# A decoder layer on one core: scores on four 32-row strips, values in one run, and a fixed order of products on TensorE

## The chip, the core and the metric

The kernel runs on one core of a Trainium2 chip. A core has TensorE (PE; its weight loads are shown apart, as PEld), VectorE (DVE), ScalarE (ACT), GpSimd (POOL) and SyncE (SP), which here only issues DMAs. TensorE writes its results into PSUM, eight banks of 128 partitions by 512 fp32 numbers; DVE and ACT read PSUM, POOL does not. The metric is the device time of one execution in microseconds, the median of the runs.

## The reference

Two sequences of 2048 tokens with 512 features go through three sublayers, each followed by a residual sum and a layer norm.

```
x = layernorm(x + ssm(x))                   # state-space layer, 16 heads of 32
x = layernorm(x + cross_attention(x, ctx))  # 16 heads of 32, 77 context tokens
x = layernorm(x + slots(x))                 # dispatch to 16 slots, 16 experts, combine
```

The change is in the second line. Its attention is

```
q = x@q_w + q_b;  k = ctx@k_w + k_b;  v = ctx@v_w + v_b       # per head 32 wide
att = softmax(causal(q @ k.T / sqrt(32)))                      # [token, 77] per head
x2  = layernorm(x + (att @ v) @ o_w + o_b)
```

and the same stage also computes the dispatch part of the third line: a running softmax over the tokens for 128 rows (16 slots times 16 heads, in two halves of 128) and the sums `Z` of `x2` weighted by it.

## The kernel before

Four stages follow one another. The first is the state-space layer; between its products, `setup()` computes the keys and values. The second, the attention stage, goes over 16 tiles of 256 tokens, each handled as two halves `s` of 128 tokens. The third runs the 16 experts, whose 192 MB of weights are streamed in 1 MB slabs by SP's queue. The last combines and writes the output.

Products that need more precision are split: an operand is kept as a high part in the format fp32r and a low remainder, and `three` adds high·high, high·low and low·high. These are single TensorE instructions. The plain fp32 products `uu`, `y`, `up` and `qp` appear in the trace as two instructions each; transposes are single ones.

In the attention stage the work of a tile `n` is cut into functions, which the text names by letters where the change does. `load` fetches the tokens and the first layer's output; `scaled` (POOL and ACT) prepares them. `out_proj` (O, per half) is 12 products with 512 columns, a residual sum and the layer norm's chain of small DVE and ACT instructions. `x1_transposed` (X, per half) is four transposes and the split. `queries` (Q, per half of the features) makes two groups of 12 products with 256 columns, both into one PSUM tile `qq`; behind each group ACT writes `qh` (L787) and DVE writes `ql` (L788) from that group's half of the tile. `weigh` (W) makes the scores of four heads: three products into one bank of `sc`, then the softmax on DVE and ACT, and a multiplication by the reciprocal on POOL (L820). `gather` (G) transposes the four heads' probabilities; `values` (V) multiplies them with the values. `o_proj` (P, per half) is 12 products with 512 columns and the second layer norm; `x2_transposed` (Y), `dispatch` (D, 24 products with 256 columns), `p_transposed` (T) and `collect` (C, twice six products with 512 columns) belong to the slots.

The keys are stored block-diagonally: for a group of four heads the right operand has 4·77 = 308 columns, and row strip `r` (32 rows, the features of head `r`) is non-zero only in its own 77 columns. One product over all 128 rows thus gives four heads' scores:

```
for k, (l, r) in enumerate(((qh, kbh[b]), (qh, kbl[b]), (ql, kbh[b]))):
    mm(sc[:, 0:4 * S], l[:, hg % 2, ss], r[:, hg, :], k == 0, k == 2)
```

Per tile there are 2 halves and 4 head groups, so 24 such products. `setup()` builds the block-diagonal keys in four blocks of two groups each: a POOL memset of `kf`, four DVE copies of 32 partitions (L443), an ACT cast and a POOL subtraction. In `values` every head's product uses 32 weight columns and writes its own 32 partitions, so that four heads use four column strips of the array; four heads make eight instructions.

The order of the calls comes from `plan` (eight lists, one tile's period), with hand-made lists for the `head` and the `drain`. The functions are called in that order, but the framework that builds the program then schedules every engine's instructions itself: it may move instructions of one engine past one another where no data dependence forbids it, and the queues of the engines hold the result, in a fixed order. Dependences on PSUM are kept by the framework.

PSUM in this stage: one bank `y`, two each for `mm`, `tr` and `sc`. `mm` serves O, Q, P, D and C in turn.

The experts' slabs `0` to `9` and `A` to `M` lie on memory that the attention stage partly still uses; `first` gives the order in which they are filled the first time, and `dwc` two slabs for two other weights (default `KL`).

Of the kernel before, what the change touches and what calls it, by code (L numbers as in the profile page):

```python
# [16 lines left out]
S = 77  # L17
NE, FF = 16, 2048
# [4 lines left out]
NT = T // TB  # L23
# [11 lines left out]
DEFPLAN = [  # L35
    ["W", "V", ["scaled", 0, 0], ["x2_transposed", 3, 1], ["queries", 1, 0], "G"],
    ["W", "V", ["scaled", 0, 1], ["dispatch", 3], "G"],
    ["W", "V", ["o_proj", 2, 0], "G"],
    ["W", "V", ["p_transposed", 3], ["queries", 1, 1], "G"],
    ["L", "W", "V", ["x2_transposed", 2, 0], ["out_proj", 0, 0], "G"],  # L40
    ["W", "V", ["out_proj", 0, 1], "G"],
    ["W", "V", ["x1_transposed", 0, 0], ["o_proj", 2, 1], "G"],
    ["W", "V", ["x1_transposed", 0, 1], ["collect", 3], "G"]]
# [33 lines left out]
def weave(flows, depth, lag):  # L77
# [3 lines left out]
    while flows or live:  # L81
# [4 lines left out]
        for f in list(live):  # L86
# [6 lines left out]
TUNED = {'plan': [['W', ['x2_transposed', 3, 1], 'V', 'G'], ['V', 'W', 'G', ['scaled', 0, 0]],  # L93
          ['G', ['out_proj', 0, 0], ['queries', 1, 0], 'W', 'V', ['dispatch', 3]], ['W', ['o_proj', 2, 0], ['queries', 1, 1], 'G', 'V'],
          ['G', 'V', 'W', ['scaled', 0, 1], ['x2_transposed', 2, 0]], ['V', ['p_transposed', 3], 'W', 'G'],
          ['W', 'V', ['out_proj', 0, 1], ['x1_transposed', 0, 0], 'G'],
          ['V', ['x1_transposed', 0, 1], ['o_proj', 2, 1], 'L', 'G', 'W', ['collect', 3]]],
 'E': {'uf': 2,
# [15 lines left out]
 'lg': 1,  # L114
 'lv': 2,
 'dv': [1, 3],
 'first': 'ABCD067451892GH3JIFEKLM',
# [63 lines left out]
 'head': [['load', 0], ['scaled', 0, 0], ['out_proj', 0, 0], ['load', 1], ['scaled', 0, 1], ['scaled', 1, 0], ['x1_transposed', 0, 0],  # L181
          ['out_proj', 0, 1], ['out_proj', 1, 0], ['x1_transposed', 0, 1], ['queries', 0, 0], ['queries', 0, 1], ['weigh', 0, 0, 0], ['load', 2],
          ['weigh', 0, 0, 2], ['gather', 0, 0, 0], ['scaled', 1, 1], ['weigh', 0, 0, 1], ['values', 0, 0, 0], ['out_proj', 1, 1], ['gather', 0, 0, 2],
          ['x1_transposed', 1, 0], ['gather', 0, 0, 1], ['values', 0, 0, 1], ['weigh', 0, 0, 3], ['x1_transposed', 1, 1], ['weigh', 0, 1, 0],
          ['values', 0, 0, 2], ['gather', 0, 1, 0], ['weigh', 0, 1, 1], ['weigh', 0, 1, 2], ['scaled', 2, 0], ['out_proj', 2, 0], ['gather', 0, 0, 3],
          ['queries', 1, 0], ['weigh', 0, 1, 3], ['values', 0, 0, 3], ['gather', 0, 1, 1], ['o_proj', 0, 0], ['gather', 0, 1, 2], ['values', 0, 1, 0],
          ['queries', 1, 1], ['scaled', 2, 1], ['weigh', 1, 0, 0], ['gather', 0, 1, 3], ['x1_transposed', 2, 0], ['weigh', 1, 0, 1],
          ['values', 0, 1, 1], ['values', 0, 1, 2], ['values', 0, 1, 3], ['x2_transposed', 0, 0], ['gather', 1, 0, 0], ['weigh', 1, 0, 2],
          ['values', 1, 0, 0], ['out_proj', 2, 1], ['gather', 1, 0, 1], ['load', 3], ['values', 1, 0, 1], ['weigh', 1, 0, 3], ['o_proj', 0, 1],
          ['x1_transposed', 2, 1], ['gather', 1, 0, 2], ['x2_transposed', 0, 1], ['weigh', 1, 1, 0], ['values', 1, 0, 2], ['gather', 1, 0, 3],  # L190
          ['scaled', 3, 0], ['values', 1, 0, 3], ['weigh', 1, 1, 1], ['gather', 1, 1, 0], ['out_proj', 3, 0], ['weigh', 1, 1, 2], ['queries', 2, 0],
          ['gather', 1, 1, 1], ['values', 1, 1, 0], ['dispatch', 0], ['o_proj', 1, 0], ['queries', 2, 1], ['weigh', 1, 1, 3], ['gather', 1, 1, 2]],
 'drain': [['values', 12, 1, 1], ['gather', 12, 1, 3], ['values', 12, 1, 2], ['weigh', 13, 0, 0], ['scaled', 14, 1], ['x2_transposed', 12, 0],
           ['values', 12, 1, 3], ['weigh', 13, 0, 1], ['p_transposed', 11], ['gather', 13, 0, 0], ['x1_transposed', 14, 0], ['weigh', 13, 0, 2],
           ['values', 13, 0, 0], ['out_proj', 14, 1], ['gather', 13, 0, 1], ['values', 13, 0, 1], ['x1_transposed', 14, 1], ['load', 15],
           ['o_proj', 12, 1], ['gather', 13, 0, 2], ['weigh', 13, 1, 0], ['weigh', 13, 0, 3], ['weigh', 13, 1, 1], ['values', 13, 0, 2],
           ['collect', 11], ['x2_transposed', 12, 1], ['gather', 13, 0, 3], ['gather', 13, 1, 0], ['values', 13, 0, 3], ['scaled', 15, 0],
           ['out_proj', 15, 0], ['gather', 13, 1, 1], ['weigh', 13, 1, 2], ['values', 13, 1, 0], ['dispatch', 12], ['queries', 14, 0],
           ['weigh', 13, 1, 3], ['gather', 13, 1, 2], ['scaled', 15, 1], ['o_proj', 13, 0], ['queries', 14, 1], ['values', 13, 1, 1],
           ['gather', 13, 1, 3], ['values', 13, 1, 2], ['weigh', 14, 0, 0], ['x2_transposed', 13, 0], ['p_transposed', 12], ['values', 13, 1, 3],  # L200
           ['weigh', 14, 0, 1], ['gather', 14, 0, 0], ['weigh', 14, 0, 2], ['values', 14, 0, 0], ['out_proj', 15, 1], ['x1_transposed', 15, 0],
           ['gather', 14, 0, 1], ['values', 14, 0, 1], ['x1_transposed', 15, 1], ['o_proj', 13, 1], ['gather', 14, 0, 2], ['weigh', 14, 0, 3],
           ['collect', 12], ['x2_transposed', 13, 1], ['weigh', 14, 1, 0], ['gather', 14, 0, 3], ['values', 14, 0, 2], ['values', 14, 0, 3],
           ['weigh', 14, 1, 1], ['queries', 15, 0], ['gather', 14, 1, 0], ['gather', 14, 1, 1], ['weigh', 14, 1, 2], ['dispatch', 13],
           ['values', 14, 1, 0], ['weigh', 14, 1, 3], ['o_proj', 14, 0], ['queries', 15, 1], ['gather', 14, 1, 2], ['values', 14, 1, 1],
           ['gather', 14, 1, 3], ['values', 14, 1, 2], ['x2_transposed', 14, 0], ['values', 14, 1, 3], ['weigh', 15, 0, 0], ['p_transposed', 13],
           ['weigh', 15, 0, 1], ['o_proj', 14, 1], ['gather', 15, 0, 0], ['weigh', 15, 0, 2], ['values', 15, 0, 0], ['gather', 15, 0, 1],
           ['weigh', 15, 0, 3], ['gather', 15, 0, 2], ['x2_transposed', 14, 1], ['values', 15, 0, 1], ['collect', 13], ['weigh', 15, 1, 0],
           ['weigh', 15, 1, 1], ['values', 15, 0, 2], ['weigh', 15, 1, 2], ['gather', 15, 0, 3], ['values', 15, 0, 3], ['gather', 15, 1, 0],
           ['gather', 15, 1, 1], ['dispatch', 14], ['values', 15, 1, 0], ['weigh', 15, 1, 3], ['o_proj', 15, 0], ['gather', 15, 1, 2],  # L210
           ['values', 15, 1, 1], ['gather', 15, 1, 3], ['x2_transposed', 15, 0], ['values', 15, 1, 2], ['values', 15, 1, 3], ['p_transposed', 14],
           ['o_proj', 15, 1], ['collect', 14], ['x2_transposed', 15, 1], ['dispatch', 15], ['p_transposed', 15], ['collect', 15]],
 'pme': 0,
 'b1': 27,
# [3 lines left out]
 'x2': 2,  # L218
 'zt': 2,
 'qb': 2}  # L220
# [3 lines left out]
def tile_decoder(ctx, tc, a, out, dbg=None, upto=9, opt=None):  # L224
# [56 lines left out]
    kbh, kbl = ([kv_[b].tile([128, 4, 4 * S], FR, name=f"kb{t}{b}") for b in range(B)] for t in "hl")  # L281
# [11 lines left out]
    with ExitStack() as st:  # L293
# [121 lines left out]
        def setup():  # L415
# [20 lines left out]
            for b in range(B):  # L436
                for h in range(2):
                    m2 = slice(2 * h, 2 * h + 2)
                    kf = sb.tile([128, 2, 4, S], FP, tag="sw", bufs=2, name="kf")
                    pool.memset(kf, 0.0)  # L440
                    for r in range(4):
                        sr = slice(32 * r, 32 * r + 32)
                        dve.tensor_copy(kf[sr, :, r, :], kst[sr, m2, b * S:b * S + S])  # L443
                    split(kbh[b][:, m2].rearrange("p m (r s) -> p m r s", s=S), kbl[b][:, m2].rearrange("p m (r s) -> p m r s", s=S), kf, pool)
                    yield
# [254 lines left out]

    with ExitStack() as st:
        psb = {tag: st.enter_context(tc.tile_pool(name="b_" + tag, bufs=n, space=PSUM, reuse_waits="tile"))
               for tag, n in (("y", 1), ("mm", 2), ("tr", 2), ("sc", 2))}
        sbq, sb1, sb0 = (st.enter_context(tc.tile_pool(name=nm, bufs=1, side="right", reuse_waits="tile"))
                         for nm in ("b_q", "b_x1T", "b_in"))
        sbz, sbx, sb = (st.enter_context(tc.tile_pool(name=nm, bufs=1, side="right", reuse_waits="tile"))
# [125 lines left out]
        def values(n, s, hg):  # L832
            b = n // NT
            if hg == 0:
                ts[n]["y", s] = PT("y", bufs=1)
# [95 lines left out]
        def period(p):  # L931

            for q8, items in enumerate(PLAN):
                for it in items:
# [8 lines left out]
                    if 0 <= op_[1] < N:  # L943
                        yield op_
# [650 lines left out]
```

## Time and profile before

| | us |
|---|---|
| median of three runs | 1507.3 (1503.42 to 1508.44) |
| the profiled execution: its own time | 1507.68 |
| its span, first to last instruction | 1505.3 |
| PE busy in the span | 1351.7 (90%) |
| DVE busy | 912.4 (61%) |
| ACT busy | 620.1 (41%) |
| POOL busy | 447.5 (30%) |
| first product of the attention stage starts | 315.4 |
| last product of the attention stage ends | about 923 |

The profiled execution took 2.4 us more than its span, and 0.4 us more than the median. The span's PE share is an average over stages: the state-space stage ends near 315 us, the attention stage runs to about 923 us, the experts to about 1400 us. In the third, the DMA engines move 408 GB/s on average and are busy 99% of the time from 925 to 1400 us; in the attention stage they move 59 GB/s.

In the lists of groups a line names the source line, engine, operation and tile (out<-in); in the timeline the first column is the start and the second the duration in us, and a bracket gives the engine's idle time before the instruction and what released it. Matmuls are pipelined, so that their durations overlap: the price of one is the distance from its start to the next start.

### The profile page before, as it was taken

Reading aid. Unit: us, or ns where it says so; the run is one execution under the profiler, and the core shown is the slowest. Engines: PE = TensorE matmul, PEld = TensorE weight load, DVE = VectorE, ACT = ScalarE, POOL = GpSimd, SP = SyncE. Lnnn points to the kernel's source line nnn. Section 1 sums busy time; section 2 is a strip of 40 time slices with the busy share of each in tenths; the row PEclk is TensorE's granted clock in tenths of the full one; section 3 lists DMA queues with packets and bytes.
Section 4 is the critical chain, followed back from the end, with each engine's and each line's share of the span. In section 5 each row is a group of like instructions: output and inputs, shape, how many; then the busy total and the mean of one; then the engine's idle time right before and its main releaser. Section 6 shows DMA issues by size and latency. Waiting matters only on the chain.

```text
span 1505.3 us, 27732 instructions
## 1 busy us (share of the span) xinstructions
PE 1351.7 (90%) x10442; PEld 994.8 (66%) x10442; DVE 912.4 (61%) x2150; ACT 620.1 (41%) x1685; POOL 447.5 (30%) x496
## 2 busy tenths in 40 slices
PE   7899999979999999999999997948987977889896
PEld 6788889867878888888888875205653544532365
DVE  7997997857788888888887764002111111134497
ACT  5534544525655566565656552001010000034256
POOL 4634543634444444444443311000000000000045
PEclk9999999988999999999999998969998998999899
DMA  9889978993212121322210249998999999999547
GB/s 319 210 196 239 231 198 213 242 273 92 72 57 63 58 63 57 92 57 65 64 43 15 71 153 358 363 416 363 399 418 420 418 418 419 418 421 420 226 145 261
DMA packets 188061, 339.64 MB, mean 226 GB/s; under 512 B 12347, under 2 KB 135739, under 8 KB 163096
## 3 DMA queue, kind: packets, MB, share of 16 engines
q1 hardware_dynamic: 171632, 311.25, 59.7%
q10 hardware_dynamic: 16296, 26.62, 5.2%
q8 instruction: 83, 1.36, 0.4%
q14 instruction: 50, 0.41, 0.1%
HBM read 299.56 MB, written 38.27 MB: 224 GB/s over the span
## 4 chain that ended last, share of the span: by engine, by line
PE 58%; DVE 17%; DMA 15%; ACT 5%; issue 3%; POOL 1%; SPq 1%; ACTq 0%; POOLq 0%; DVEq 0%
PE mm L231 26%; DMA ew<-in_e_W 10%; PE up L231 6%; PE pj L231 4%; PE tr L828 3%; DVE X L530 3%; PE yac L231 3%; PE sc L231 3%; PE y L231 2%; DMA ew<-in_e_Wg 2%; PE fo L231 1%; PE uu L231 1%; DVE C L530 1%; PE gp L231 1%; ACT pp L818 1%
## 5 line engine op out<-in xcount | busy, mean ns | idle before, releaser
L231 PE MATMUL up<-ew,hT 128*32 128x512 f32 x944 | 131.3, 639 | 35.5 <-DMA ew<-in_e_W 32.1
L820 POOL TENSOR_TENSOR pp<-pp,den 128x308 f32<-128x308 f32 x128 | 89.4, 703 | 158.6 <-DVE den L819 106.2
L1185 POOL MEMSET aT<- 128x512 f32 x16 | 8.3, 524 | 404.7 <-PE yac L231 403.0
L1176 ACT ACTIVATE sv<-up 128x512 f32<-128x512 f32 x32 | 19.1, 597 | 247.2 <-PE up L231 234.2
L231 PE MATMUL mm<-xTh,cqh 128*128 128x256 f32 x256 | 76.3, 308 | 26.1 <-ACT xTh L234 26.1
L231 PEld LDWEIGHTS up<-ew,hT 128*32 128x32 f32 x944 | 27.2, 113 | 101.8 <-issue 66.0
L1235 DVE TENSOR_TENSOR Qc<-mm,vec 128x512 f32<-128x512 f32 x32 | 22.1, 691 | 113.3 <-PE mm L231 113.3
L242 DVE TENSOR_TENSOR xTl<-tr,xTh 128x512 fp32r<-128x512 f32 x32 | 21.3, 689 | 109.2 <-ACT xTh L234 109.1
L828 PE MATMUL tr<-cst,pp 128*77 128x128 f32 x512 | 81.9, 285 | 1.9 <-DVE x1Tl L724 1.2
L234 ACT COPY pt<-tr 77x512 f32<-77x512 f32 x96 | 55.7, 583 | 63.2 <-PE tr L828 35.4
L231 PE MATMUL mm<-x1Th,w30h 128*128 128x256 f32 x256 | 76.7, 301 | 5.0 <-ACT x1Th L723 2.6
L818 ACT ACTIVATE pp<-sc,mx 128x77 f32<-128x77 f32 x240 | 75.5, 327 | 12.2 <-DVE mx L815 11.4
L231 PEld LDWEIGHTS mm<-xTh,cqh 128*128 128x128 f32 x256 | 51.3, 205 | 40.4 <-ACT xTh L234 29.5
L231 PE MATMUL mm<-xTl,cqh 128*128 128x256 f32 x256 | 76.6, 301 | 1.2 <-DVE xTl L242 1.2
L231 PE MATMUL mm<-x1Tl,w30h 128*128 128x256 f32 x256 | 74.4, 291 | 0.5 <-DVE x1Tl L724 0.5
L231 PE MATMUL mm<-xTh,cql 128*128 128x256 f32 x256 | 74.8, 294 | 0.0
L231 PE MATMUL mm<-x1Th,w30l 128*128 128x256 f32 x256 | 73.8, 288 | 0.0
L828 PEld LDWEIGHTS tr<-cst,pp 128*77 128x77 f32 x512 | 60.5, 150 | 16.8 <-issue 11.1
L530 DVE SCALAR_TENSOR_TENSOR X<-raw,vec,X 128x256 f32<-128x256 f32 x80 | 66.4, 876 | 5.5 <-ACT X L526 5.0
L231 PE MATMUL yac<-ew,aT 128*32 128x512 f32 x488 | 65.1, 652 | 4.7 <-issue 4.2
L746 POOL TENSOR_TENSOR ut<-ut,fb 128x512 f32<-128x512 f32 x32 | 41.2, 1291 | 73.7 <-DMA ut<-Ud 43.2
L242 POOL TENSOR_TENSOR yyl<-ut,yyh 128x512 fp32r<-128x512 f32 x32 | 41.1, 1285 | 68.3 <-ACT yyh L234 67.5
(376 smaller groups left out, 4329.2 us busy)
## 6 DMA issues: line engine op xcount, KB each, us to landing
ew<-in_e_W SPq DMA_DIRECT2D x119, 1024.0 KB, 15.0
ew<-in_e_Wg SPq DMA_DIRECT2D x60, 1024.0 KB, 12.9
BS<-scrBc SPq DMA_DIRECT2D x48, 256.0 KB, 4.9
CS<-scrC SPq DMA_DIRECT2D x48, 256.0 KB, 6.3
xs<-in_xT SPq DMA_DIRECT2D x32, 256.0 KB, 5.7
xt<-in_x SPq DMA_DIRECT2D x32, 256.0 KB, 2.7
ut<-Ud SPq DMA_DIRECT2D x32, 256.0 KB, 3.3
fb<-fd SPq DMA_DIRECT2D x128, 64.0 KB, 3.1
```

Of the source, the lines that this page charges most:

```text
L231: return pe.matmul(o, lhsT=l, rhs=r, start=start, stop=stop, **kw)
L234: (act.copy, dve.tensor_copy, pool.tensor_copy)[e](o, i)
L242: (lo_eng or dve).tensor_tensor(lo, src, hi, ALU.subtract)
L530: dve.scalar_tensor_tensor(dst, raw[:, j, 1 + t:1 + t + TB], w4[:, t:t + 1], dst, ALU.mult, ALU.add)
L746: (act, dve, pool)[EN.get('uf', 1)].tensor_tensor(ut, ut, fb, ALU.mult)
L818: act.activation(pp[:, r, :], sv[:, r, :], AF.Exp, bias=mx[:, h:h + 1], accum_out=den[:, h:h + 1])
L820: (act, dve, pool)[EN.get('d%d' % hg, 2)].tensor_tensor(pp, pp, den[:, h4].unsqueeze(2).to_broadcast([128, 4, S]), ALU.mult)
L828: pe.transpose(tp[0:S, r * 128:r * 128 + 128], pp[:, r, :], ident)
L1176: last["silu"] = act.activation(sv, up, AF.Silu)
L1185: pool.memset(aT, 0.0)
L1235: dve.tensor_tensor(Qc[b][:, mp * 2:mp * 2 + 2, t1:t1 + TB], qq, vec[:, V_CQ + mp * 2:V_CQ + mp * 2 + 2].unsqueeze(2).to_broadcast([128, 2 ...
```

## The change

The keys are stored densely, four heads in the 128 rows and 80 columns (77 and three of padding) for each group; `kf` is built with one memset, one DVE copy of 128 partitions and one split per sequence. `weigh` handles all four groups of a half at once: each score product now uses 32 rows, one head's features, against 80 columns, and the four heads of a group lie on four row strips of the array and write to four different banks. `sc` takes four banks, once. `values` handles a half's 16 heads in one call, with its result in an `mm` bank. `collect` is split into two calls. The order of the stage's products is a string of letters, 37 for the beginning, 13 times a period of 26, and 41 for the end; from the thirteenth letter on, every TensorE instruction is tied to the one before it, so that TensorE's order is the string's order, also inside a letter. `queries`, `out_proj`, `o_proj`, `dispatch` and the transposes are unchanged inside. Loads follow the O letters. The number of buffers for `x2` goes from 2 to 4, for `pt` from 3 to 5, and the slabs' first order and `dwc` change.

```diff
-    kbh, kbl = ([kv_[b].tile([128, 4, 4 * S], FR, name=f"kb{t}{b}") for b in range(B)] for t in "hl")
+    kbh, kbl = ([kv_[b].tile([128, 4, SP], FR, name=f"kb{t}{b}") for b in range(B)] for t in "hl")
...
-                    kf = sb.tile([128, 2, 4, S], FP, tag="sw", bufs=2, name="kf")
-                    pool.memset(kf, 0.0)
-                    for r in range(4):
-                        sr = slice(32 * r, 32 * r + 32)
-                        dve.tensor_copy(kf[sr, :, r, :], kst[sr, m2, b * S:b * S + S])
...
+                kf = sb.tile([128, 4, SP], FP, tag="sw", bufs=2, name="kf")
+                pool.memset(kf, 0.0)
+                dve.tensor_copy(kf[:, :, 0:S], kst[:, :, b * S:b * S + S])
+                split(kbh[b], kbl[b], kf, pool)
+                yield
...
-               for tag, n in (("y", 1), ("mm", 2), ("tr", 2), ("sc", 2))}
+               for tag, n in (("mm", 2), ("tr", 2))}
+        scp = st.enter_context(tc.tile_pool(name="b_sc", bufs=1, space=PSUM, reuse_waits="tile"))
...
+        def weigh(n, s):
...
+            sc = scp.tile([128, 4, 512], FP, tag="sc", bufs=1, name="sc")
+            for g in range(4):
+                qh, ql = ts[n]["q", g // 2]
+                for k, (l, r_) in enumerate(((qh, kbh[b]), (qh, kbl[b]), (ql, kbh[b]))):
+                    for r in range(4):
+                        sr = slice(32 * r, 32 * r + 32)
+                        mm(sc[:, r, g * SP:g * SP + SP], l[sr, g % 2, ss], r_[sr, g, :], k == 0, k == 2)
+            for hg in range(4):
+                h4 = slice(hg * 4, hg * 4 + 4)
+                sv = sc[:, :, hg * SP:hg * SP + S]
...
+        def values(n, s):
...
+            yp = PT("mm")
+            for g in range(4):
+                pt = ts[n].pop(("pt", s, g))
+                for r in range(4):
+                    h = g * 4 + r
+                    mm(yp[32 * r:32 * r + 32, g * 128:g * 128 + 128], vt[b][:, 32 * h:32 * h + 32], pt[:, r, :], True, True)
...
+ORDER = ("OOXOXQQWGOGGGWVXOXPGGGQGQVYWPGOGGGYVW"
+         + 13 * "XODXPGGQGGQVTYWPCGOGGCGYWV"
+         + "XDXPGGQGGQVTYWPCGGGCGYWVDPGGGGVTYPCCYDTCC")
...
+            if at_ >= opt.get("pin", 12):
+
+                new = [i for i in traced[since:] if i.engine == mybir.EngineType.PE]
+                before = [i for i in traced[:since] if i.engine == mybir.EngineType.PE][-1:]
+                for p_, i_ in zip(before + new, new):
+                    tc.add_manual_dep(i_, p_.name, mybir.DependencyInfo(mybir.DependencyClass.NoSync, mybir.DependencyReason.DATA),
+                                      reason="order")
```

## The prediction

> **What bounds the kernel now.** The busy time by stage comes first (columns: us; busy time and count of PE, PEld, DVE, ACT, POOL; granted clock; DMA share; GB/s).
>
> ```profile
> 444.00:870.00 426.00, 422.04 (x3233) 356.76 (x3232) 346.81 (x920) 254.68 (x857) 177.75 (x185) 1.00 0.20 59
> 925.00:1400.00 475.00, 391.67 (x2912) 195.42 (x2911) 94.08 (x186) 69.96 (x114) 7.75 (x15) 0.91 0.99 408
> ```
>
> From 444 to 870 us the attention stage does twelve tiles at 35.5 us each, and PE is busy 422 of 426 us, DVE 347. PE is the bound. From 925 us the weight stream is. SP's queue shows why the two ends move together:
>
> ```profile
> SPq L1052 <- PE up L231: 19.6, 6, 14.2
> ```
>
> This is from 905 to 960 us: once the slabs are full, the next load waits for the experts' first products, and these wait for the attention stage's last one. So I pass a change of that stage's end on one to one.
>
> Next PE's timeline, because a price here is the distance between starts.
>
> ```profile
> 524.10 0.31 PE L231 MATMUL sc<-kbh,qh 128*128 128x308 f32 x1
> 524.24 0.30 PE L231 MATMUL sc<-kbl,qh 128*128 128x308 f32 x1
> ...
> 528.35 0.39 PE L231 MATMUL mm<-x2h,dtl 128*128 128x512 f32 x1
> 528.67 0.43 PE L231 MATMUL y<-pt,vt 77*32 77x128 f32 x8
> 529.02 0.66 PE L828 MATMUL tr<-cst,pp 128*77 128x128 f32 x4
> 529.44 0.39 PE L231 MATMUL sc<-kbh,qh 128*128 128x308 f32 x1
> 529.67 0.31 PE L231 MATMUL sc<-kbl,qh 128*128 128x308 f32 x1
> ...
> 548.23 0.39 PE L231 MATMUL mm<-w32h,yvl 128*128 128x512 f32 x1
> 548.55 0.86 PE L231 MATMUL y<-pt,vt 77*32 77x128 f32 x24
> 549.34 0.38 PE L231 MATMUL mm<-x1Th,w30h 128*128 128x256 f32 x1
> 549.56 0.28 PE L231 MATMUL mm<-x1Tl,w30h 128*128 128x256 f32 x1
> ```
>
> A score product costs 0.14, a product of 256 columns 0.12, of 512 columns 0.23, a transpose 0.109. Entering and leaving a run of `y` costs extra: from 528.35 to 529.67 are 1.32 us, of which one 512-column product, four transposes and one score product explain 0.81; the eight `y` took 0.51. From 548.23 to 549.56, less 0.23 and 0.12, the 24 took 0.98. So an instruction costs (0.98-0.51)/16 = 0.029 and a run 0.28 whatever its length. A window of twelve tiles has 78 runs, 6.4 a tile.
>
> Check of a tile: 24 O and 24 P products and 12 of C at 0.23 (13.8), 72 of Q and D at 0.12 (8.6), 24 scores (3.4), 52 transposes (5.7), 64 `y` (1.9), 6.4 runs (1.8): 35.2. Nothing is left over: PE hardly ever stalls.
>
> Why not, where `queries` writes both groups of 12 products into one bank and reads the first between? Because PE does other work there:
>
> ```profile
> 465.23 0.28 PE L231 MATMUL mm<-x1Th,w30l 128*128 128x256 f32 x1
> 465.36 0.60 PE L721 MATMUL tr<-cst,x 128*128 128x128 f32 x4
> 465.88 0.43 PE L231 MATMUL y<-pt,vt 77*32 77x128 f32 x8
> 466.24 0.66 PE L828 MATMUL tr<-cst,pp 128*77 128x128 f32 x4
> ...
> 467.28 0.47 DVE L788 SCALAR_TENSOR_TENSOR ql<-mm,vec,qh 128x256 fp32r<-128x256 f32 x1
> ...
> 467.81 0.39 PE L231 MATMUL mm<-x1Th,w30h 128*128 128x256 f32 x1 [0.63 <-DVE ql L788]
> ```
>
> The twelfth product starts at 465.23, four other groups follow, and then PE idles 0.63 us until `ql` of the first group is written; the second group starts 0.06 us later. In all 32 calls the second group starts only after the first group's `ql`. The scheduler filled the gap with other letters' work.
>
> **The change, part by part.** The sum is made against the profiled execution's own 1507.7 us.
>
> Q under a fixed order. TensorE's order is now tied inside a letter too, so nothing may come between the two groups. What is queued behind the waiting product is all of PE's later work. In the row above `ql` was late because DVE was occupied; in another call it follows at once:
>
> ```profile
> 515.70 0.28 PE L231 MATMUL mm<-x1Th,w30l 128*128 128x256 f32 x1
> ...
> 516.02 0.48 ACT L787 ACTIVATE qh<-mm,vec 128x256 fp32r<-128x256 f32 x1 [0.20 <-PE mm L231]
> ...
> 516.53 0.48 DVE L788 SCALAR_TENSOR_TENSOR ql<-mm,vec,qh 128x256 fp32r<-128x256 f32 x1 [0.26 <-ACT qh L787]
> ```
>
> From the twelfth start to the end of `ql` are 1.32 us, and 1.33 or less in 20 of the 32 calls. Less the 0.12 that the next product would have started after anyway, and with 0.05 for the release, the stall is 1.25 us. Two of the 32 calls stand among the first twelve letters, which are free: 30 x 1.25 = +37.5 us. Less it cannot be, as both instructions must run; at the row of 465, 467.81-465.23-0.12 = 2.5 us, it would be +74. I take the shortest, which is the commonest.
>
> Values in one run. Two runs a tile replace 6.4: 4.4 x 0.28 x 16 = -19.7 us. The 64 instructions stay.
>
> Scores. 24 products at 0.142 (3.4 us a tile) become 96 on row strips, 24 groups of four. No product before uses row strips. The nearest row is the four column strips of `y`: eight instructions at 0.029, so four in 0.118, with starts 7 ns apart. That gives 24 x 0.118 = 2.83, -0.58 a tile, -9.3 us. From below: a stream of 80 columns at the score product's rate (0.142/308) is 0.037 a group, -40 us. From above: a product on its own weights never came closer than 0.111, even with 16 columns,
>
> ```profile
> 266.81 1.96 PE L231 MATMUL qp<-sqTs,dwq 128*128 128x16 f32 x16
> ```
>
> (15 distances in 1.96 less the last one's 0.29), so if strips don't overlap, 96 x 0.111 = 10.7, +116 us. I take 0.118, as four tiles of the array at once is what the row shows.
>
> Here a rule speaks against the change. The Trainium skill, "TensorE: Matmul & The Clock Gate", section "LDWEIGHTS (loading the stationary operand)", says that a load takes its columns divided by 1.2 per ns, and that one of 32 rows takes as long as one of 128. A strip's load would then be no cheaper than the whole one, 107 ns by that figure as an estimate, and 96 of them one after another would make 10.3 us a tile and some 1640 us in all; the same page's Part 3 lets loads on other row groups overlap, which gives about the sum below. The 0.111 row agrees with the first figure; no row here shows a strip of rows.
>
> Entering the strips. W makes two runs a tile. If they cost what a `y` run costs, 32 x 0.28 = +9.0 us; the other end is 0, as the products may count as full-width ones. I take 0.28, the only row.
>
> Setup of the keys. The chain from 120 to 200 us has 8.6% on `kf` L443, 6.9 us; sixteen DVE copies become two of 308 columns at some 0.47 (the row `pp` L811 of that size). But PE is busy 77.7 of those 80 us and is late next. I take -4; ends 0 and -7.
>
> Costed at nothing: the softmax has the same instructions, ACT 255 and DVE 347 of 426 us, covered by PE while PE is longer; `collect` split in two; loads, which SP issues two products earlier at least; more buffers. Beginning and end of the stage: the order there is fixed too. The chain of the last tile (O, norm, transposes, D, T, C) is the same; its lists were free to interleave before. I take 0, with -8 to +15 for it.
>
> Sum: 37.5 - 19.7 - 9.3 + 9.0 - 4 = +13.5. 1507.7 + 13.5 = **1521 us**; the median of the runs shown lies 0.4 below the execution used.
>
> **Rivals.**
>
> Faster: the strips cost only their streams. At 0.037 a group instead of 0.118 the 384 groups give another -31: 1490 us. It decides from 13.5/384 = 0.035 below my price, 0.083 a group. For it: `y` starts its strips 7 ns apart, so issue is no bound. Against it: 0.111 for 16 columns says that loading the weights is.
>
> Slower than I say: `sc` is now one tile of four banks, so the second W of a period waits until the first one's softmax has read all of it. Between the two lie P, C, G, O, G, G, C, G, Y: 2.8+1.4+0.4+2.8+0.9+1.4+0.4+0.4 = 10.5 us, 13.4 with W itself. DVE's work there: one half's softmax (reductions and subtractions at 0.47, reciprocals 0.17: 4.4), two norm chains (2.3 and 3.1 with `x1`), two Z at 0.73, copies of 0.67 and 0.69: 12.7 us. DVE just fits, if it never waits for ACT's exponentials (0.31 each, eight of them). An overrun of 1.7 us a tile is +25: 1546 us.
>
> Much slower: strips load one after another, +125 over my term: 1646 us. The trace has no row against it but the column strips.
>
> The order isn't in force: if the ties are only hints, the second Q group is still covered and 37.5 goes: 1484 us. Against it: a tie is a dependence, and dependences are what kept Q's groups apart above.
>
> **How the numbers follow.** Chances: my case 0.55, with its own range of 1508 to 1537 from the ends of setup, strip entry and stage ends; faster strips 0.17; `sc` late 0.16; serial loads 0.08; order not in force 0.04. The range of 1490 to 1556 leaves out serial loads, the unforced order and a little on both sides, together under 0.2. Within 0.3%, 4.5 us, a measurement can't tell the kernel from no change. Slower by more: 0.43 of my case, 0.16, 0.08 and 0.01: 0.68. Faster: 0.03 of my case, 0.13 and 0.04: 0.20. The rest, 0.12, is the same.
>
> **What would show it.** After each Q's twelfth product PE idles about 1.2 us, released by `ql`, once a call. `y` comes in two runs a tile of 32. The `sc` starts come in fours, a group every 0.12 us. `sc` waits released by DVE or ACT inside W's first product would speak for the second rival, groups of 0.44 us for the third, PE busy throughout Q for the fourth. The prediction is wrong if the period of 26 letters is not near 35.5 + 2.5 - 1.2 - 0.6 + 0.6 = 36.8 us, or if the end of the stage doesn't move the end of the kernel.

## The result and the profile after

The changed kernel takes 1628.1 us in the median (1626.0 to 1631.0), the kernel before beside it 1507.2 (1503.4 to 1508.4): 1.081 times as long, with an interval of 1.078 to 1.084. Forecast were 1521 us and at most 1556. The profiled execution took 1629.2 us over a span of 1627.1.

| us | before | after |
|---|---|---|
| first product of the attention stage | 315.4 | 322.0 |
| its last product ends | 922.9 | 1051.4 |
| last product with `up` | 1401.1 | 1524.6 |
| span | 1505.3 | 1627.1 |
| a tile (starts of D, third to twelfth) | 35.62 | 44.08 |

All of the loss arises before 1051 us, and nearly all in the attention stage, whose length goes from 607.5 to 729.4 us. Stretches of the changed kernel, with the columns of the prediction's first fence (the first is nine tiles, the second the experts):

```profile
498.00:894.70 396.70, 330.35 (x3096) 280.23 (x3096) 269.10 (x693) 199.00 (x644) 141.49 (x145) 0.97 0.17 48
1060.00:1520.00 460.00, 380.20 (x2852) 188.92 (x2856) 92.49 (x180) 67.44 (x110) 7.82 (x15) 0.92 1.01 415
```

PE, busy 422 of 426 us before, is now busy 330 of 397, and at a clock of 0.97. DVE's work is nearly what it was (269.1/9 = 29.9 us a tile, 346.8/12 = 28.9 in the prediction's window), so the waits are new, not the work. The experts' stretch is no longer than before (458.3 us from its first to its last product with `up`, 462.8 before), and at its start SP's queue waits as before (from 1030 to 1090 us):

```profile
SPq L970 <- PE up L193: 18.7, 7, 14.2
```

So the question is the attention stage alone. The list of PE's waits in the same nine tiles (engine and line, what it waited for: us in all, times, longest):

```profile
PE mm L193 <- DVE ql L747: 26.7, 18, 2.0
PE mm L193 <- DVE yvl L204: 10.0, 9, 2.3
PE mm L193 <- DVE zt L812: 6.8, 9, 1.4
PE tr L788 <- DVE nb L849: 6.6, 7, 1.0
PE tr L680 <- DVE bmv L649: 6.1, 6, 1.3
PE mm L193 <- ACT pd L852: 3.9, 8, 0.5
PE mm L193 <- DVE zt L716: 3.4, 6, 0.7
```

The first line is Q's inner wait, 18 times, two a tile as forecast: the first of a tile idles 1.92 to 1.97 us in eight of nine tiles, the second 1.08 or 1.09 in all nine. The next six, 36.8 us or 4.1 a tile, were not forecast. They are spread over six letters (D, O, G, X or Y, Q, P): a `mm` or `tr` bank, or an operand, is ready late because VectorE or ScalarE is late. None of them is W waiting for `sc`.

PE's timeline at one Q (start, length, instruction; in the bracket the idle time before it and its cause):

```profile
597.65 0.28 PE L193 MATMUL mm<-x1Tl,w30h 128*128 128x256 f32 x1
597.77 0.28 PE L193 MATMUL mm<-x1Th,w30l 128*128 128x256 f32 x1
600.01 0.58 PE L193 MATMUL mm<-x1Th,w30h 128*128 128x256 f32 x1 [1.97 <-DVE ql L747]
600.39 0.41 PE L193 MATMUL mm<-x1Tl,w30h 128*128 128x256 f32 x1
600.61 0.41 PE L193 MATMUL mm<-x1Th,w30l 128*128 128x256 f32 x1
600.82 0.41 PE L193 MATMUL mm<-x1Th,w30h 128*128 128x256 f32 x1
...
603.86 0.36 PE L193 MATMUL mm<-x1Th,w30h 128*128 128x256 f32 x1
604.06 0.28 PE L193 MATMUL mm<-x1Tl,w30h 128*128 128x256 f32 x1
604.18 0.28 PE L193 MATMUL mm<-x1Th,w30l 128*128 128x256 f32 x1
```

Ahead of the stall the same product starts every 0.12 us, behind it every 0.21, and from 604 us on every 0.12 again: the clock is at half for 3.4 us. The nine tiles have seven such pieces; before had none from 470 to 790 us.

The strips themselves are cheap. One W of the changed kernel:

```profile
579.75 0.31 PE L193 MATMUL sc<-kbh,qh 32*128 32x80 f32 x4
579.88 0.29 PE L193 MATMUL sc<-kbl,qh 32*128 32x80 f32 x4
579.99 0.29 PE L193 MATMUL sc<-kbh,ql 32*128 32x80 f32 x4
580.10 0.29 PE L193 MATMUL sc<-kbh,qh 32*128 32x80 f32 x4
```

A group of four costs 0.11 us, so four strips do run at a time. Adding up the distances from start to start in nine tiles (idle time taken off), TensorE's price per tile is, in us:

| | scores | values | G | other transposes | Q | O, P, D, C | idle | tile |
|---|---|---|---|---|---|---|---|---|
| before | 3.84 | 2.62 | 3.28 | 2.03 | 5.99 | 17.60 | 0.26 | 35.62 |
| after | 2.94 | 2.02 | 4.26 | 2.61 | 7.24 | 17.64 | 7.37 | 44.08 |

Scores and values together save 1.5 us a tile. Idle time takes 7.1, and half clock most of Q's 1.25. The idle time begins at a product's modelled end, 0.16 us after the next one could have started, and so much of every stall is counted with the letter ahead of it. With half clock and the way into the strips this is most of what G and the other transposes take more (1.56 us). What holds VectorE behind the W above shows in its own timeline, and the last line is the product that waits for it:

```profile
582.28 0.55 DVE L722 TENSOR_SCALAR x<-zt,brs 128x512 f32<-128x512 f32 x1
582.74 0.47 DVE L775 TENSOR_REDUCE mx<-sc 128x4 f32<-128x308 f32 x1
584.74 0.18 DVE L779 RECIPROCAL den<-den 128x4 f32<-128x4 f32 x1 [1.53 <-ACT pp L778]
584.84 0.45 DVE L770 TENSOR_REDUCE mx<-sc 128x4 f32<-128x308 f32 x1
585.39 0.48 DVE L771 TENSOR_TENSOR pp<-sc,mx 128x308 f32<-128x308 f32 x1
585.78 0.47 DVE L775 TENSOR_REDUCE mx<-sc 128x4 f32<-128x308 f32 x1
586.17 0.68 DVE L204 TENSOR_TENSOR yvl<-mm,yvh 128x512 fp32r<-128x512 f32 x1
...
586.90 0.39 PE L193 MATMUL mm<-x2Th,kqh 128*128 128x256 f32 x1 [1.25 <-DVE yvl L204]
```

It takes the first group's maximum, and then its next instruction is that group's reciprocal, which needs ScalarE's exponentials: 1.53 us of idling, while the scores of three more groups lie ready. Behind the reciprocal stand instructions of two more groups, and only then `yvl`, the reading that frees a bank of `mm`. What `yvl` needs from ScalarE was ready at 585.12 us, and PE idles 1.25 us ahead of D's first product until `yvl` is done.

### The profile page after: what moved, and what is told of

Its sections match the earlier page's. It is cut to its first block, busy times and chain, and to the rows that moved or that the text cites. A ratio compares the mean times of both kernels' runs of the same rounds, so it can differ in the third digit from the quotient of the medians.

```text
span 1627.1 us, 29978 instructions
## 1 busy us (share of the span) xinstructions
PE 1369.8 (84%) x11594; PEld 1017.3 (63%) x11594; DVE 912.6 (56%) x2136; ACT 631.0 (39%) x1683; POOL 444.3 (27%) x492
## 4 chain that ended last, share of the span: by engine, by line
PE 43%; DVE 26%; DMA 16%; ACT 8%; issue 4%; POOL 2%; ACTq 0%; DVEq 0%; POOLq 0%; SPq 0%
PE mm L193 15%; DMA ew<-in_e_W 10%; PE pj L193 5%; PE up L193 5%; DMA ew<-in_e_Wg 4%; PE yac L193 2%; DVE X L488 2%; PE uu L193 2%; ACT pp L778 2%; PE gp L193 2%; POOL pp L780 2%; PE tr L788 2%; DVE bst L648 2%; DVE brs L653 1%; PE sc L193 1%
## 5 line engine op out<-in xcount | busy, mean ns | idle before, releaser
L193 PE MATMUL mm<-x1Th,w30h 128*128 128x256 f32 x256 | 83.8, 328 | 48.6 <-DVE ql L747 41.3
L788 PEld LDWEIGHTS tr<-cst,pp 128*77 128x77 f32 x512 | 67.5, 161 | 38.6 <-issue 15.0
L193 PEld LDWEIGHTS mm<-x1Th,w30h 128*128 128x128 f32 x256 | 53.6, 210 | 58.1 <-DVE ql L747 48.6
L193 PE MATMUL mm<-x1Tl,w30h 128*128 128x256 f32 x256 | 78.0, 305 | 0.4 <-DVE x1Tl L683 0.4
L204 POOL TENSOR_TENSOR x2l<-x,x2h 128x512 fp32r<-128x512 f32 x32 | 41.0, 1281 | 135.0 <-ACT x2h L196 135.0
L193 PE MATMUL mm<-x1Th,w30l 128*128 128x256 f32 x256 | 77.7, 303 | 0.0
L747 DVE SCALAR_TENSOR_TENSOR ql<-mm,vec,qh 128x256 fp32r<-128x256 f32 x64 | 30.8, 481 | 72.9 <-ACT qh L746 72.9
```

The source lines that it names most:

```text
L193: return pe.matmul(o, lhsT=l, rhs=r, start=start, stop=stop, **kw)
L204: (lo_eng or dve).tensor_tensor(lo, src, hi, ALU.subtract)
L747: dve.scalar_tensor_tensor(ql[:, q, :], o, bq, qh[:, q, :], ALU.add, ALU.subtract)
L788: pe.transpose(tp[0:S, r * 128:r * 128 + 128], pp[:, r, :], ident)
```

## The experiments

All are kernels of their own; "1560" and the like are medians in us. A change of a few us in them means little: two of the programs below (the first and the one with the softmax spread) turned out to be the same on every engine, and gave 1559.7 and 1554.4.

**Q's readings behind both groups.**

```diff
                 three(o, lambda k: qw_h[:, k, ms], ...)
+            for q in range(2):
+                m = mp * 2 + q
+                o = qq[:, q * TB:q * TB + TB]
                 bq = vec[:, V_QB + m:V_QB + m + 1]
                 act.activation(qh[:, q, :], o, AF.Identity, bias=bq)
```

> The changed kernel, but in the step Q all 24 products are issued ahead of ScalarE's and VectorE's readings, so that TensorE does not wait between the two groups of one bank. Theory 'the fixed order exposes Q's own wait': the two stalls a tile (about 1.45 us each) go, and with them the 3.4 us at half clock that followed one of them in most periods (about 2 us a tile); the period falls from 44.1 to about 39 us and the time from 1628 to about 1550 us (15 tiles x 4.9). Rival 'the softmax on one four-bank tile bounds the period': the waits move to the steps behind Q, the period stays above 43 us, the time above 1605 us.

Measured: 1559.7 us, period 39.36, clock 1.00. The first theory's numbers, within 10 us. PE's waits now:

```profile
PE mm L193 <- DVE zt L815: 12.8, 9, 1.7
PE mm L193 <- DVE yvl L204: 7.2, 10, 2.4
PE mm L193 <- ACT pd L855: 5.6, 7, 1.6
```

`ql` is gone from the head of the list, the half-clock pieces are down from seven to one, and over 4 us of idling a tile stay.

**TensorE's order left to the scheduler.**

```diff
- 'pin': 12,
+ 'pin': 10**6,
```

> The changed kernel, with the dependences that fix TensorE's order left out, so that the compiler's scheduler places the same products as it did in the kernel before. Theory 'fixed order': the period comes back to about 35 us and the time to 1490 to 1515 us. Rival 'softmax on one four-bank tile' (or the one bank fewer that V now takes from the pair called mm): the period stays above 41 us, the time above 1580 us.

Measured: 1559.7, period 38.92: between the two. A free order takes off as much as the last edit, and far from all.

**Both edits.**

> Both earlier edits on the changed kernel: TensorE's order left to the scheduler, and Q's readings behind all its products. Each alone took 68 us off (1628 to 1560). Theory 'both edits remove the same thing, the wait inside Q': together they give no more than one, 1550 to 1565 us. Rival 'the fixed order costs more than Q's wait': the gains add in part, under 1540 us.

Measured: 1543.5. They largely remove the same thing; the remaining 16 us are the most that a fixed order cost beyond Q's wait.

**Full-width scores in one step.** In place of the strips, each group's three products of 320 columns go to a bank of its own:

```diff
-                    for r in range(4):
-                        sr = slice(32 * r, 32 * r + 32)
-                        mm(sc[:, r, g * SP:g * SP + SP], l[sr, g % 2, ss], r_[sr, g, :], k == 0, k == 2)
+                    mm(sc[:, g, 0:4 * SP], l[:, g % 2, ss], r_.rearrange("p g s -> p (g s)"), k == 0, k == 2)
...
```

With dense keys such a product mixes the four heads of a group. These three runs, and the one with dense keys alone further down, therefore leave out what keeps the heads apart: they give prices and are no versions of the layer.

> The changed kernel with its fixed order, but a head group's scores are three full-width products of 320 columns into a bank of its own, in place of twelve strip products over four banks; keys, buffers and order are untouched. (Its scores mix the four heads of a group, so the output is another one.) Theory 'fixed order': the period stays at 44 us or grows by 1 us (24 products of about 0.15 us a tile against 2.5 us of strips), time 1620 to 1645 us. Rival 'four head groups in the same four banks hold up the softmax': VectorE and ScalarE no longer alternate on one tile, the period falls under 41 us, the time under 1585 us.

> The changed kernel, order fixed, Q's readings behind all its products, and the full-width scores with a bank for each head group (the output is another one: the four heads of a group are mixed). Theory 'the four-bank tile accounts for part of what was left': the waits on the bank of the pair mm are half gone (VectorE is through the softmax earlier), the period falls from 39.4 to about 37.5 to 38 us and the time from 1560 to 1525 to 1540 us. Rival 'V in the pair mm accounts for it, whatever the scores': the period stays at 39 us or over, 1550 to 1575 us.

> As the last, with TensorE's order left to the scheduler too: against the kernel before there remain the dense keys' 320 columns, the four groups of scores in one step, the values in one run in a bank of the pair mm, and the sequence of steps (the output is another one, as before). Theory 'strips and their four shared banks are what the free order cannot hide': within 1495 to 1520 us. Rival 'values in the pair mm and the new sequence': 1535 us or more.

Measured: 1600.1 with Q as changed, 1543.9 with its readings behind, 1539.5 with a free order too. Although TensorE's score time rises from 2.94 to 3.8 to 4.3 us a tile, the kernel is 28 and 16 us faster than with strips. So the strips together with their four shared banks cost more than they save. Which of the two it is, no run shows. The order of VectorE's queue differs as well: in the traces with Q's readings behind, two of a tile's four readings `zt` (of O's and P's banks) stand behind the maxima of all four groups of a half with strips, in each of nine tiles, and behind two or three of them with full width, in 17 of 18 cases. And 34 to 39 us over the kernel before (1505.2 beside these runs) stay; the last run says that the fixed order does not hold them. By its expectation the new sequence of letters would; the runs with four steps below refute that.

**Parts of the change on the kernel before.** Values in one run in a `mm` bank (at the place of the fourth):

```diff
-            if hg == 0:
-                ts[n]["y", s] = PT("y", bufs=1)
...
+            if hg == 3:
+                ts[n]["y", s] = yp = PT("mm")
+                for g in range(4):
...
```

> The kernel before with one part of the change alone: the 16 value products of a half in one run (on its list, at the place of the fourth), into a bank of the pair mm, with six buffers for the transposed weights. Theory 'the run is worth 0.6 us a tile on TensorE and the bank it takes from the other products costs as much or more': 1505 to 1540 us, with waits for a bank of mm showing in the list of waits. Rival 'the run is a plain gain, as forecast': 1488 to 1499 us.

Measured: 1507.4, ratio 1.0004 (0.9982 to 1.0026). Values fall from 2.62 to 2.38 us a tile, scores rise from 3.84 to 4.19. Neither loss nor gain.

On top of it, a half's four groups weighed in one step, full width (`weigh` returns for `hg > 0` and loops over the groups for `hg == 0`; the tile's second `queries` is drawn ahead):

> The kernel before with its own list and free order, where a half's four head groups are weighed in one step (at the place of the first, the second half of the queries drawn ahead of it, four banks for scores) and its values are one run in the pair mm; block-diagonal keys and full-width scores stay. Theory 'the new sequence of steps loses the time, not their size': 1500 to 1520 us. Rival 'four groups of softmax in one burst hold up VectorE and ScalarE': 1530 us or more.

Measured: 1540.9, the rival's side. The next run takes the step back and keeps the queries drawn ahead:

> The kernel before with its values in one run (1507) and, besides, only the second half of a tile's queries drawn ahead of its first weighing, as the run with all four groups in one step (1541) had it too. Theory 'the one step made the 34 us': 1505 to 1515 us. Rival 'the queries drawn ahead made them': 1530 us or more.

Measured: 1507.6. The queries cost nothing; the one step made the 33 us.

With dense keys, strips and one four-bank `sc` as well:

> As the last, and the scores are the changed kernel's: dense keys, strips of 32 rows, one tile of four banks that all four groups share. So this is every part of the change but its letters and their fixed order (and the buffers of x2). Theory 'shared banks cost about what the strips save': within 12 us of the last run. Rival 'strips under a free order, among other products, with the softmax on shared banks': 25 us or more above it (strips 4.1 us a tile instead of 3.8, and a period longer by 1.5 us).

Measured: 1667.4, 126 above the full-width scores in one step (1540.9), five times the rival's least. TensorE idles 5.4 us a tile, mostly in transposes that wait for weights and values that wait for transposed ones, and its clock is 0.89 on average, so that O and Q take 2.9 us a tile more than before. The new letters suit the strips better (1628, and 1560 with a free order) than the old list does.

The dense keys' building alone:

```diff
-    kbh, kbl = ([kv_[b].tile([128, 4, 4 * S], FR, name=f"kb{t}{b}") for b in range(B)] for t in "hl")
+    kbh, kbl = ([kv_[b].tile([128, 4, SP], FR, name=f"kb{t}{b}") for b in range(B)] for t in "hl")
...
-                mm(sc[:, 0:4 * S], l[:, hg % 2, ss], r[:, hg, :], k == 0, k == 2)
+                mm(sc[:, 0:4 * SP], l[:, hg % 2, ss], r.rearrange("p g s -> p (g s)"), k == 0, k == 2)
```

> The kernel before with the dense keys' building alone; its scores are still full-width products, of 320 columns (and so mix the four heads of a group: the output is another one). Theory 'the shorter key setup moves stage 1 earlier, as forecast': the attention stage's first product at 311 to 315 us (315.4 before). Rival 'it puts stage 1's steps in another order and makes it later, as in the changed kernel': 318 us or later, the whole 3 to 8 us longer than before.

Measured: 1505.0 (ratio 1.0007, 0.9981 to 1.0034); the stage's first product at 316.3 us. Neither theory: the keys' building moves nothing.

The order of the old list made fixed (the change's own tie, from the 101st step):

> The kernel before (block-diagonal keys, values by head group, its own list of steps) with TensorE bound to the order of that list from the 101st step to the end of the stage, which takes in all tiles but the first two or three. Theory 'fixed order': each of about 26 Q steps now shows its inner wait of 1.25 to 1.5 us and other waits come on top; the time rises from 1507 by 35 to 120 us. Rival 'the new scores and their tile': the order alone costs little, the time stays under 1520 us.

Measured: 1725.5, with a period of 57.5 us and a clock of 0.84 over six tiles. Far above the theory's range. A list made for a scheduler that may deviate from it is a bad fixed order; this says nothing of what a string made for it costs.

**W taken apart into four steps.** `weigh` handles one group, with the kernel before's keys and a bank for each group; at W's place stands the first, the others follow one by one behind the next letters:

```diff
-         + 13 * "XODXPGGQGGQVTYWPCGOGGCGYWV"
+         + 13 * "WXWOWDXPGGQGGQVTYWPWCWGWOGGCGYWV"
...
-        steps = dict(O=(out_proj, 2), ..., W=(weigh, 2), ...
+        steps = dict(O=(out_proj, 2), ..., W=(weigh, 8), ...
```

> The changed kernel with Q's readings behind its products, and W taken apart again: each head group is weighed in a step of its own, full width from block-diagonal keys into a bank of its own, and the three further steps stand one by one between the next steps of the fixed order (at W's place the first). All other letters stay, order fixed. Theory 'four groups in one step hold up the softmax and what stands behind it': 1560 falls to 1505 to 1525 us, the period to 35.5 to 36.5 us. Rival 'the sequence of the other letters and its fixed order': as with full-width scores in one step, 1535 to 1550 us, period over 37.3 us.

> The same with TensorE's order left to the scheduler. Theory 'four groups in one step': 1500 to 1520 us, near the kernel before. Rival 'sequence of letters': 1530 us or more, as the free order with one step (1540).

> The changed kernel with W alone taken apart into four steps (full width, block-diagonal keys, a bank each, order fixed); Q's readings stay between its two groups of products. Theory 'two causes that add': 1628 less some 52 us, 1570 to 1585 us, with Q's inner wait of about 1.2 to 1.5 us, 18 times in nine tiles, still there. Rival 'Q's wait costs so much only while VectorE is held by four groups of softmax at once': the wait shrinks under 0.8 us each and the time is under 1545 us.

Measured: 1508.3 with Q's readings behind and a fixed order (ratio 1.0022, 1.0003 to 1.0042), 1503.3 with a free one (1.0003, 0.9983 to 1.0023), 1552.8 with Q's readings between its groups and a fixed order. The first two settle it: the fixed order costs about 5 us against a free one, and the letters' sequence with it 3 us against the kernel before (1505.3 beside these runs). PE's waits and VectorE's first lines in nine tiles of the first:

```profile
PE mm L193 <- ACT pd L857: 5.6, 6, 1.5
PE tr L793 <- POOL pp L785: 2.5, 2, 2.0
PE mm L193 <- DVE ql L753: 0.4, 1, 0.4
```

```profile
DVE ql L753 <- ACT qh L752: 24.4, 31, 1.7
DVE den L784 <- ACT pp L783: 10.3, 18, 0.9
```

VectorE's wait for the exponentials is 10.3 us here. In one step it was, over nine tiles of the changed kernel and of the one-step run with full-width scores and Q's readings behind:

```profile
DVE den L779 <- ACT pp L778: 30.8, 28, 1.6
```

```profile
DVE den L780 <- ACT pp L779: 26.4, 17, 1.9
```

So on this list the wait goes with the one step, whatever the banks. It is not the price of the step by itself: on the old list it is as long without the one step (first line, the run with the queries drawn ahead, 1507.6 us) as with it (second line, 1540.9 us).

```profile
DVE den L819 <- ACT pp L818: 19.7, 17, 1.5
```

```profile
DVE den L822 <- ACT pp L821: 20.6, 16, 1.7
```

Nor does TensorE pay for the step in one place. With strips it waits for banks that VectorE reads late (`zt` and `yvl` in the lists above); with full-width scores in one step and Q's readings behind, its list has two lines, and the longer one is transposes that wait for weights:

```profile
PE tr L789 <- POOL pp L781: 17.4, 17, 1.8
PE mm L193 <- ACT pd L853: 7.7, 8, 1.3
```

PE's waits in the third run, with only Q's wait left:

```profile
PE mm L193 <- DVE ql L750: 26.1, 18, 2.2
PE tr L790 <- POOL pp L782: 3.0, 4, 2.0
PE mm L193 <- ACT pd L854: 2.8, 3, 1.1
```

The wait is what it was (26.7 us in the changed kernel), yet it costs 44.6 us (1552.8 less 1508.3) in place of 68.3. Neither theory: the two causes add, and something comes on top. All six cells, order fixed:

| scores | Q read between | Q read behind | difference |
|---|---|---|---|
| one step, strips, shared banks | 1628.1 | 1559.7 | 68 |
| one step, full width | 1600.1 | 1543.9 | 56 |
| four steps, full width | 1552.8 | 1508.3 | 45 |
| first less last | 75 | 51 | |

**Three trials at the order.** With Q's readings behind, the softmax of a half written group by group behind the next four letters:

```diff
-            for hg in range(4):
+            def softmax(hg):
...
+            late.extend((softmax, hg) for hg in range(4))
```

> The changed kernel with Q's readings behind its products (1560 us) and, besides, the softmax of a half written group by group behind the next four steps of the order, in place of all four behind W. Theory 'what is left is VectorE's queue: the readings that free a bank of mm stand behind four groups of softmax': waits on zt, yvl and nb shrink from 2.6 to about 1 us a tile, period 37.5 to 38 us, time 1530 to 1545 us. Rival 'the softmax itself is late, and later the more it is spread': the waits of the transposes on the weights grow, 1555 us or more.

Measured: 1554.4, and it tested nothing: on DVE, ACT, POOL and PE the trace has the same instructions in the same order as without the edit. Moving lines was not enough to make the scheduler order the other engines differently. Whether VectorE's order alone could be mended stays open.

With four steps, G behind O, which also puts the fourth W there (`"XWVOWDWXPGGQGGQVTYWPWCWOWGGCGGYW"`):

> As the first of these, order fixed, with the first half's transposes G all behind O and its values V one step later, so that weights and their copies have 3 to 4 us more. Theory 'with four steps the order is only short of time between a weighing and its transposes': below the first of these by 5 to 15 us, 1490 to 1510 us. Rival 'the waits are on the banks of mm': no change to the first within 5 us, or slower.

Measured: 1584.3, against the first theory, and the rival's "slower" has another cause. The timeline of POOL and PE shows it:

```profile
642.67 1.26 POOL L708 TENSOR_TENSOR ut<-ut,fb 128x512 f32<-128x512 f32 x1 [3.17 <-DMA ut<-Ud]
643.88 0.70 POOL L785 TENSOR_TENSOR pp<-pp,den 128x308 f32<-128x308 f32 x1
...
644.64 1.14 PE L793 MATMUL tr<-cst,pp 128*77 128x128 f32 x4 [5.54 <-POOL pp L785]
```

O issues the next tile's load and its first step on POOL, `ut`. The fourth group's multiplication is now behind it in POOL's queue, so the weights, whose sums are ready at 640.6, wait for a DMA.

The third G ahead of the first Q (`"...PGGGQGQV..."`), four steps otherwise as above:

> As the run with four steps, Q's readings behind its products and the order fixed (1508 us), with one letter moved: the third G of a half stands ahead of the first Q, so that Q's wait for the bank that the dispatch weights' exponentials read (0.63 us a tile) is covered by 0.45 us of transposes. Theory 'that wait is short of time only': 1508 less 5 to 8 us, 1498 to 1504 us, less than before by 0.1 to 0.5%. Rival 'the weights for the third G are late then': the wait comes back as one of the transposes on weights, 1506 us or more.

Measured: 1514.1 (ratio 1.0058, 1.0036 to 1.0080). The rival's time, but not its cause: the wait on `pd` is gone, and PE's first wait is one on ScalarE's copy of transposed weights:

```profile
PE tr L793 <- ACT pt L196: 9.3, 9, 2.0
```

Three G in a row need a third `tr` bank before ScalarE has copied the first. No version beats the kernel before; the best is level with it.

## Why the prediction was wrong

**Where it failed: "Costed at nothing: the softmax has the same instructions".** It has, and VectorE's busy time agrees. But four groups made ready at one moment put what TensorE waits for late into the other engines' queues, as the `yvl` above shows for one product. Without Q's wait, the one step costs 35.6 us with full-width scores and 51 with strips on shared banks; with it, 47 and 75; on the old list 33. That the step makes it is shown by the runs on both lists. By what way is open: no edit shows it, late banks and late weights are read from the traces, and VectorE's wait for the exponentials can't be all of it, as the old list has it without a loss. The second rival had the place and the sign, at 0.16. Its condition for VectorE, no wait for the exponentials, failed (30.8 us in nine tiles). But its way was another (a second W waiting for `sc`, which no list of the changed kernel and its variants shows), and its 1.7 us a tile was too little: the one step alone makes the tile 2.1 us longer in the full-width runs (37.57 against 35.49), with strips 3.9 (39.36).

**Q under the fixed order: +37.5.** The mechanism, the count and the place were right: two stalls a tile, `ql` their cause. The size holds for one of the two. The forecast counts a stall from 0.12 us after the twelfth start, 0.16 earlier than the idle time in the list. Counted so, the second stall of a tile is 1.24 or 1.25 us, as forecast, and the first 2.07 to 2.12 in eight of nine tiles. In these eight `qh` stands in ScalarE's queue behind a step of P's norm that waits for VectorE:

```profile
598.79 0.29 ACT L651 ACTIVATE brs<-bmv,epsc 128x1 f32<-128x1 f32 x1 [1.52 <-DVE bmv L649]
598.99 0.46 ACT L746 ACTIVATE qh<-mm,vec 128x256 fp32r<-128x256 f32 x1
599.48 0.48 DVE L747 SCALAR_TENSOR_TENSOR ql<-mm,vec,qh 128x256 fp32r<-128x256 f32 x1 [0.72 <-ACT qh L746]
```

The prediction had a longer row too (2.5 us, at 465) and took the shortest for all 30. Half clock came with the long stalls: alone the term is 44.6 us. In the changed kernel it is 68, inside the bound of 74 by luck. Per tile the two causes together make 1.16 us more than apart (44.08 - 39.36 - 39.05 + 35.49). Half clock is at most half of that: seven pieces in nine tiles, one without Q's wait, four without the one step, one without both. The rest is open.

**Values in one run: -19.7.** TensorE saves 0.6 us a tile (2.62 to 2.02), not 1.23, and in time nothing: the run on the old list measures no gain. So 4.4 runs fewer saved 0.14 us each, half the 0.28 that I had taken from two places.

**Scores: -9.3, entering the strips: +9.0.** A group of four took 0.11 us, near the 0.118 of the column strips. The score products save 0.9 us a tile, 14 us in all. Entering costs 0.17 (with Q's readings behind, the last transpose ahead of W takes 0.20 us, before W of full width 0.03), 32 times, 5.6 us. So TensorE's part in scores and entering is some -9 where the sum had 0. Unforecast was that strips, with a bank for each strip that all groups share, came out 16 to 28 us dearer in one step than full-width scores.

The Trainium skill, "TensorE: Matmul & The Clock Gate", section "LDWEIGHTS (loading the stationary operand)", which I had set against the change, does not decide here: loads one after another at its estimate would be 10.3 us a tile; 2.94 were measured, and the four loads of a group start 3 to 4 ns apart in the trace, so loads for different row strips do overlap.

**Setup of the keys: -4.** 0 by the run with dense keys alone. In the changed kernel the attention stage starts 6.6 us late; in all runs with dense keys and one step it starts at 317.6 us or later, in the others at 317.5 or earlier, and the two equal programs have 320.0 and 317.9. Why is open.

**The order otherwise: 0.** 5 us with four steps. **End of stage to end of kernel, one to one:** the stage ends 128.5 us later, the span 121.8; right but for 7 us.

## What to carry to other kernels

Adding up an engine's work tells nothing of a step that makes much work ready at once: look who waits for whom inside the burst, and what else stands in these queues behind it. A fixed order is not slow in itself (5 us here), but every wait inside a step then stands in the open: issue all of a step's products before the first reading of their bank. When two causes are suspected, measure all four combinations: here the one alone costs 45 us and the other 51, and together they cost 120.

## What the runs showed of the hardware

The granted clock changes on a grid of 3.41 us, and in the nine tiles of the changed kernel half clock lasts one such window at a time. There, 109 windows began at full clock. Seven were followed by one at half clock, and these are the seven in which PE idled longest, 1.92 to 1.96 us; the longest without a drop is 1.71. In six of the seven the idling is one long stall of Q, in the seventh a part of the 2.3 us that D waited for `yvl`. Two more long stalls of Q (1.92 and 1.94 us) lie across a border of the grid, with 1.46 and 1.26 us on their longer sides, and no drop followed. Over the same nine tiles of all twenty traces every window with 1.92 us or more was followed by half clock, none with less than 1.28 us, and between them it went both ways. Two windows of the changed kernel, before and after the drop at the Q shown above (the first figure behind the comma is PE's busy time, the clock is the third figure from the end):

```profile
596.56:599.98 3.42, 1.49 (x12) 1.28 (x11) 2.52 (x8) 1.45 (x5) 0.29 (x1) 1.00 0.25 62
599.80:603.20 3.40, 3.19 (x15) 3.19 (x16) 0.76 (x5) 1.03 (x2) 0.00 (x0) 0.53 0.12 18
```

So a tile's second stall of Q, 1.08 us, brought no drop here, and its first, 1.9 us and over, costs up to 1.7 us more (half of 3.41) when it falls whole into one window. The Trainium skill, "TensorE: Matmul & The Clock Gate", section "HAM oscillation — how this bites in real kernels", puts the rule as no idle gap of PE over about 3.4 us. This case differs: no gap in the changed kernel's list of waits above is over 2.3 us.
